# Turning and squaring the last four token tiles by channel chunk in a two-layer WKV/MoE kernel

## The chip, the cores and the metric

The kernel runs on one core of a Trainium2 chip. The core has a matrix engine (PE, with its weight loads shown apart as PEld), a vector engine (DVE), an activation engine (ACT), a general engine (POOL), and SP, which here only issues transfers. Each engine works through a queue of its own in order, and waits on semaphores that the others raise. The metric is the time of one execution on the device in microseconds (us); lower is better.

## What is computed

Input `x` is 4 x 512 x 512 (2048 tokens of 512 channels). Two layers follow one another, each a bidirectional WKV mixing and then a mixture of experts with a shared expert, each added to `x`. Cut to what matters here, the first layer is:

```python
# WKV: two decaying scans over time of exp(k) and exp(k)*v, then
num = nf + nb - ekv + euk * vf
den = df + db - ek + euk
z   = sigmoid(r) * (num / max(den, 1e-8)) * (0.8 + 0.2 * tf)
# experts
h      = z * rsqrt(mean(z * z, axis=-1) + 1e-6) * rms_weight
probs  = softmax(h @ router_w)                       # 8 experts
topv, topi = top_k(probs, 2)
moe    = sum of the two chosen experts, weighted by topv / sum(topv)
shared = silu(h @ sw_gate) * (h @ sw_up) @ sw_down
x      = x + moe + shared
```

The second layer has the same WKV and 32 experts, 6 chosen per token. The change lies in the passage of layer 0 from WKV to experts: it concerns `mean(z * z)` and `h @ router_w` of the last 512 tokens.

## The kernel before

The tokens are cut into four blocks of 512 (`b`), each into four tiles of 128 (16 tiles in all, `NT`), and the channels into four chunks of 128 (`c`). A *unit* `n` is one chunk of one block, 16 in all, worked on in the transposed layout (channels on partitions, tokens along the row). All queues have an order written out by hand: within an engine, instructions run in the order of the program text.

The main loop (line 697) has one pass per unit. For unit 15, the last, it issues the following.

- `mid(15)` (463): multiplications and four scans on DVE.
- `sums(14)` and, behind the loop, `sums(15)` (473): eight matmuls on PE, for `den` and `num`, and three activations on ACT that form `r`, the reciprocal of `den`.
- `back(14)` and, behind the loop, `back(15)` (486): four DVE operations that finish a unit's `z` in `zT`.
- `route_pos(2)` (578): two small matmuls of block 2 into the bank `pos2`. `route_slots(2)` (604), at the end of the pass on DVE, computes slot numbers from it (`slot_numbers`; lines 368 and 377 read the bank), and `write_slots(2, 8)` sends eight indirect writes on POOL.
- The shared expert of tiles 6, 7 and 8: `share_up` (PE), `share_silu` (ACT), `share_hid` (DVE).

Behind the loop come the router's steps for block 3 (lines 781 to 855). `last_channels` (787) adds one chunk to the logits `lgb` (line 789) and transposes that chunk of each tile in `pz` (line 791). `squares` (795) squares a range of columns of a tile on ACT and sums each token's squares into a column of `parts`. `share_turn(6)`, `share_down(6)` and `share_put(6)` turn the hidden rows of tile 6, multiply them by the down weights, and write the rows out. `lgT` is the logits' copy in SBUF, which PE turns back into token rows (line 821). Then `route_v`, `route_max`, `route_top`, `route_pos`, `route_pay` and `route_slots` compute the routing of block 3 on DVE with short steps on ACT and PE. `row_out` (515) copies a tile's rows and writes them to `z0d`. `write_slots` sends the last eight writes, `read_table` reads the finished table, and the experts' loop (`routed`, 872) gathers its rows by that table. Pieces of the shared expert for tiles 7 to 12 are laid between these steps.

Matmul results lie in eight PSUM banks handed out under tags:

```python
    banks.update(pool=ps, tr=2, den=2, num=1, g=2, pl=1)
```

A bank asked for under a tag is given once a bank of that tag has been read for the last time; the instruction that first writes it waits for this. In the kernel before, `pz` of tiles 12 and 13 take both `tr` banks and are turned and squared chunk by chunk (chunks 0 to 2 together, chunk 3 after `back(15)`); tiles 14 and 15 take the `num` bank and a `g` bank, and are turned whole (line 814) and squared whole after chunk 3. The single `pl` bank was last used by `pos2`; the two `g` banks by the shared expert's tiles 7 and 8.

Of the kernel before, what the change touches and what calls it, by code (L numbers as in the profile page):

```python
# [19 lines left out]
P = 128  # L20
# [13 lines left out]
def adaln_ffn_kernel(  # L34
# [26 lines left out]
    nc = tc.nc  # L61
    B, S, D = x.shape
# [4 lines left out]
    NC = D // P  # L67
    TB = S // P
    NT = T // P
# [17 lines left out]
    zT = big.tile([P, NC, T], F32, name="zT")  # L87
# [9 lines left out]
    def bank(tag, name):  # L97
        return banks["pool"].tile([P, 512], F32, tag=tag, name=name, bufs=banks[tag])


    ident = const.tile([P, P], F32, name="ident")
# [325 lines left out]
    def zcols(n):  # L427
        b, c = units[n]
        return zT[:, c, b * S : (b + 1) * S]
# [43 lines left out]
    def sums(n):  # L473

        b, c = units[n]
        den, num = bank("den", f"den{n}"), bank("num", f"num{n}")
        for p, m, (d, o) in zip((den, num), (ident, nfac[:, b, :]), mids.pop(n)):
            nc.tensor.matmul(p, m, d, start=True, stop=False)
            nc.tensor.matmul(p, m, o, start=False, stop=True)
        r = wk.tile([P, S], F32, tag="r", name=f"r{n}")  # L480
        nc.scalar.activation(r, den, AF.Relu, bias=neg_min)
        nc.scalar.activation(r, r, AF.Ln, bias=pos_min)
        nc.scalar.activation(r, r, AF.Exp, scale=-1.0)
        mids[n] = den, num, r

    def back(n):

        den, num, r = mids.pop(n)
        t = wk.tile([P, S], F32, tag="t", name=f"t{n}", bufs=1)
        nc.vector.scalar_tensor_tensor(t, den, DEN_MIN, r, ALU.max, ALU.mult)  # L490
        nc.vector.scalar_tensor_tensor(t, t, 2.0, r, ALU.subtract, ALU.mult)
        nc.vector.tensor_tensor(t, num, t, ALU.mult)
        nc.vector.tensor_tensor(zcols(n), zcols(n), t, ALU.mult)
# [147 lines left out]
    def share_turn(t, ph=None):  # L641
        if ph is None:
            ph = bank("tr", f"sph{t}")
        for f, _ in CH0:
            nc.tensor.transpose(ph[:, f : f + P], shared_hid[t][:, f : f + P], ident)
        hT = spool.tile([P, F0], F32, tag="hT", name=f"shT{t}")
        nc.scalar.copy(hT, ph[:, :F0])
        shared_hid[t] = hT

    def share_down(t, tag=None, po=None):  # L650
        dv, hT = shared0[2], shared_hid.pop(t)
        if po is None:
            po = bank(tag, f"so{t}")
        for j, (f, _) in enumerate(CH0):
            nc.tensor.matmul(po, hT[:, f : f + P], dv[:, j, :], start=(j == 0), stop=(j == len(CH0) - 1))
        shared_up[t] = po
# [40 lines left out]
    for n in range(NU):  # L697
        b, c = divmod(n, NC)
# [81 lines left out]

    bl = NB - 1
    lgb = bank("den", "lgb")
    pz = {t: bank("tr", f"pz{t}") for t in (NT - 4, NT - 3)}
    parts = wk.tile([P, 2, TB], F32, name="ssq_parts", bufs=1)
    nc.vector.memset(parts, 0.0)

    def last_channels(cs):
        for c in cs:
            nc.tensor.matmul(lgb[:E0], rout[:, c, :], zcols(bl * NC + c), start=(c == 0), stop=(c == NC - 1))
            for t, p in pz.items():  # L790
                nc.tensor.transpose(p[:, c * P : (c + 1) * P], zT[:, c, t * P : (t + 1) * P], ident)
# [3 lines left out]
    def squares(t, lo, hi, part):  # L795
        nc.scalar.activation(
            sq[:, lo:hi], pz[t][:, lo:hi], AF.Square, accum_out=parts[:, part, t - bl * TB : t - bl * TB + 1]
        )

    last_channels((0, 1))  # L800
    sums(NU - 1)
    last_channels((2,))
    for t in pz:
        squares(t, 0, D - P, 0)
    po = bank("g", "so_6")
    share_turn(6, po)
    back(NU - 1)
    share_down(6, po=po)
    last_channels((NC - 1,))
    lgT = wk.tile([E0, S], F32, tag="lgT", name="lgT_last", bufs=1)  # L810
    for t, tag in ((NT - 2, "num"), (NT - 1, "g")):
        pz[t] = bank(tag, f"pz{t}")
        for c in range(NC):
            nc.tensor.transpose(pz[t][:, c * P : (c + 1) * P], zT[:, c, t * P : (t + 1) * P], ident)
    squares(NT - 4, D - P, D, 1)
    squares(NT - 3, D - P, D, 1)
    nc.scalar.copy(lgT, lgb[:E0])
    squares(NT - 2, 0, D, 0)
    squares(NT - 1, 0, D, 0)
    for i in range(TB):  # L820
        nc.tensor.transpose(lgb[:, i * E0 : (i + 1) * E0], lgT[:, i * P : (i + 1) * P], ident[:E0, :E0])
    routes[bl] = lgb
# [425 lines left out]
    with tc.manual_schedule(  # L1248
# [6 lines left out]
        f, m = FCH[LAST]  # L1255
# [13 lines left out]
        for n in range(2 * NB):  # L1269
            b, t = n // 2, 2 * n + TB  # L1270
# [26 lines left out]
    for h in range(NHALF):  # L1297
# [3 lines left out]
        for b in range(NB):  # L1301
# [12 lines left out]
            for i in range(TB):  # L1314
                t = b * TB + i
                po = bank("tr", f"o{n}_{i}")
# [50 lines left out]
```

## Time and profile before

| what | value |
|---|---|
| median of 3 runs | 1504.74 us (1502.43 to 1507.55) |
| the profiled execution | 1499.05 us |
| its span in the trace | 1497.3 us |
| PE busy over the span | 93% |
| mean granted PE clock | 0.981 of full |
| DVE busy | 46% |
| ACT busy | 27% |
| POOL busy | 38% |
| start of the first logits matmul of block 3 (line 789) | 186.90 us |
| start of the first expert matmul (line 971) | 237.20 us |

The times are of the device. The table's last two rows bracket the stretch that the change touches: some 50 us out of 1497. Before it lies the WKV of layer 0, after it the experts of layer 0, then layer 1. Positions in the trace are counted from the start of the span. In the timelines of the profile, a row gives start, duration, engine, line, operation, output and inputs, count, and in brackets how long the engine was idle before it and who released it; matmuls overlap, so a row's duration is a little longer than its distance to the next.

### The profile page before, as it was taken

The page shows a single profiled execution, that of the slowest core. Times are in us where ns is not written, and L with a number is a line of the kernel's source. Part 1 is how long each engine was busy: PE and PEld are TensorE (multiplying, and loading weights), DVE is VectorE, ACT ScalarE, POOL GpSimd, SP SyncE. Part 2 cuts the span into 40 slices and gives each one's busy share as a digit, 9 for nine tenths or more (in the row PEclk, how much of TensorE's full clock was granted, in tenths as well). Part 3 has the DMA queues.
Part 4 walks back from the last instruction along what each step waited for, and adds up shares of the span by engine and source line. Part 5 has one row for each costly group of instructions (what it writes and reads, how often), then busy time and mean ns, then how long its engine had stood idle before and what let it go on. Part 6 is the DMA issues. An engine that isn't in the chain of part 4 may idle for free. (4 is left out here: it accounts for less than half of the span.)

```text
span 1497.3 us, 16067 instructions
## 1 busy us (share of the span) xinstructions
PE 1388.2 (93%) x4927; PEld 820.1 (55%) x4927; DVE 692.6 (46%) x1260; ACT 398.3 (27%) x962; POOL 573.6 (38%) x564
## 2 busy tenths in 40 slices
PE   5788888988788799999999999999999999999997
PEld 3455456766556454444445555555555555555554
DVE  7999949999980358511112222222222222222221
ACT  5666544444344251000001111111111111111110
POOL 1010245666564001555543343434343344343322
PEclk8999999999999999999999999999999999999999
DMA  8311216464545731010136654666456575546442
GB/s 301 99 54 51 78 58 188 77 132 99 131 104 124 244 132 52 1 58 29 56 110 187 153 142 115 169 170 194 103 131 182 142 231 155 142 129 165 111 96 40
DMA packets 118188, 184.71 MB, mean 123 GB/s; under 512 B 19864, under 2 KB 64940, under 8 KB 118040
## 3 DMA queue, kind: packets, MB, share of 16 engines
q1 hardware_dynamic: 82216, 125.28, 24.7%
q0 software_dynamic: 35296, 56.63, 20.2%
q8 instruction: 66, 1.08, 0.3%
q10 hardware_dynamic: 528, 1.05, 0.2%
q14 instruction: 82, 0.67, 0.1%
HBM read 151.02 MB, written 52.64 MB: 136 GB/s over the span
## 5 line engine op out<-in xcount | busy, mean ns | idle before, releaser
L946 PE MATMUL pout<-w,hT 128*128 128x512 f32 (+1 forms) x432 | 200.4, 596 | 1.3 <-DVE hT L939 0.8
L951 POOL DMA_INDIRECT out_dram<-kA,put x52 | 83.1, 1597 | 279.2 <-DVE kA L950 147.9
L905 POOL DMA_INDIRECT acc<-z1d,put x119 | 123.7, 1039 | 123.1 <-PE pza L918 63.2
L987 DVE SCALAR_TENSOR_TENSOR hrow<-pup,tab,sgt 128x352 f32<-128x352 f32 x84 | 49.1, 584 | 249.7 <-issue 127.4
L398 POOL DMA_INDIRECT table<-pay,r1sloti x96 | 95.1, 991 | 172.3 <-ACT sg L1309 111.7
L950 DVE COPY kA<-pout 128x512 f32<-128x512 f32 x84 | 58.1, 692 | 176.0 <-PE pout L946 164.1
L971 PE MATMUL pgate<-w,kA 128*128 128x352 f32 x416 | 132.8, 462 | 6.0 <-PEq L1032 5.9
L975 PE MATMUL pup<-w,kA 128*128 128x352 f32 x416 | 131.6, 459 | 0.0
L946 PEld LDWEIGHTS pout<-w,hT 128*128 128x128 f32 (+1 forms) x432 | 76.6, 191 | 67.6 <-issue 53.8
L986 ACT ACTIVATE sgt<-pgate 128x352 f32<-128x352 f32 x84 | 39.0, 464 | 250.5 <-PE pgate L971 245.4
L971 PEld LDWEIGHTS pgate<-w,kA 128*128 128x128 f32 x416 | 75.3, 190 | 49.8 <-issue 16.4
L918 PEld LDWEIGHTS pza<-ident,acc 128*128 128x128 f32 x584 | 72.3, 142 | 51.3 <-issue 33.5
L975 PEld LDWEIGHTS pup<-w,kA 128*128 128x128 f32 x416 | 77.4, 190 | 39.7 <-issue 0.2
L918 PE MATMUL pza<-ident,acc 128*128 128x128 f32 x584 | 87.4, 275 | 10.6 <-DMA acc<-z0d,put 8.5
L398 POOL DMA_INDIRECT table<-r0pay,r0sloti x32 | 34.7, 1085 | 158.8 <-DVE r0sloti L389 110.5
L928 ACT COPY kA<-pza 128x256 f32<-128x256 f32 x103 | 38.3, 372 | 205.8 <-DVE kA L927 156.7
L905 POOL DMA_INDIRECT acc<-z0d,put x51 | 68.1, 1335 | 58.4 <-PE pgate L971 18.6
L946 PE MATMUL pout<-zT,hT 128*128 128x512 f32 (+1 forms) x192 | 87.8, 592 | 0.0
L1153 PE MATMUL g<-zT,w 128*128 128x512 f32 (+1 forms) x192 | 86.5, 593 | 0.0
L1153 PE MATMUL u<-zT,w 128*128 128x512 f32 (+1 forms) x192 | 86.3, 592 | 0.0
L1318 PE MATMUL o<-w,kA 128*128 128x512 f32 (+1 forms) x192 | 84.5, 593 | 0.0
L971 PE MATMUL pgate<-zT,kA 128*128 128x352 f32 x256 | 81.3, 460 | 2.0 <-PEq L1032 2.0
(301 smaller groups left out, 2205.3 us busy)
## 6 DMA issues: line engine op xcount, KB each, us to landing
w<-in_L_ffn_w_dram SPq DMA_DIRECT2D x44, 704.0 KB, 5.8
zT<-in_L_ffn_w_dram SPq DMA_DIRECT2D x20, 704.0 KB, 5.8
w<-in_L_ffn_w_dram SPq DMA_DIRECT2D x22, 512.0 KB
zT<-in_L_ffn_w_dram SPq DMA_DIRECT2D x10, 512.0 KB
w<-in_L_ffn_w_dram SPq DMA_DIRECT2D x22, 192.0 KB, 8.6
acc<-in_x_dram SPq DMA_DIRECT2D x4, 1024.0 KB, 9.1
xa<-acc SPq DMA_DIRECT2D x4, 1024.0 KB
z0d<-zr SPq DMA_DIRECT2D x16, 256.0 KB, 2.0
```

Of the source, the lines that this page charges most:

```text
L398: ins = nc.gpsimd.indirect_dma_start(out=table, out_offset=bass.IndirectOffsetOnAxis(ap=sloti[:, t, j : j + 1], axis=0), in_=pay[:, t, j, ...
L905: nc.gpsimd.indirect_dma_start(out=rows(e, s), out_offset=None, in_=zd, in_offset=bass.IndirectOffsetOnAxis(ap=put_at[:, e * NS + s : e * ...
L918: nc.tensor.transpose(pza[which][:, c * P : (c + 1) * P], rows(e, s)[:, c * P : (c + 1) * P], ident)
L946: nc.tensor.matmul(po, hT[:m, j, :], dv[:m, j, :], start=(j == 0), stop=(j == nf - 1))
L950: nc.vector.tensor_copy(row, po)
L951: nc.gpsimd.indirect_dma_start(out=outs(n), out_offset=bass.IndirectOffsetOnAxis(ap=at, axis=0), in_=row, in_offset=None, bounds_check=T - ...
L971: nc.tensor.matmul(pg, zt[:, c, :], gv[:, c, :], start=(c == 0), stop=(c == NC - 1))
L975: nc.tensor.matmul(pu, zt[:, c, :], uv[:, c, :], start=(c == 0), stop=(c == NC - 1))
L986: nc.scalar.activation(sgt, pg, AF.Silu)
L987: nc.vector.scalar_tensor_tensor(hrow, pu, tab[:, col, 1:2], sgt, ALU.mult, ALU.mult)
L1153: nc.tensor.matmul(p[: m + more], wv[:, c, f : f + m + more], zT[:, c, b * S : (b + 1) * S], start=(c == 0), stop=(c == NC - 1),)
L1318: nc.tensor.matmul(po, hid[:m, j, i * P : (i + 1) * P], dv[:m, j, :], start=(j == 0), stop=(j == len(FCH) - 1))
```

## The change

```diff
     lgb = bank("den", "lgb")
-    pz = {t: bank("tr", f"pz{t}") for t in (NT - 4, NT - 3)}
+    pz = {bl * TB + i: bank(g, f"pz{bl * TB + i}") for i, g in enumerate(("tr", "tr", "pl", "g"))}
...
     last_channels((0, 1))
     sums(NU - 1)
     last_channels((2,))
+    po = bank("g", "so_6")
+    share_turn(6, po)
     for t in pz:
         squares(t, 0, D - P, 0)
-    po = bank("g", "so_6")
-    share_turn(6, po)
     back(NU - 1)
+    last_channels((NC - 1,))
     share_down(6, po=po)
-    last_channels((NC - 1,))
     lgT = wk.tile([E0, S], F32, tag="lgT", name="lgT_last", bufs=1)
-    for t, tag in ((NT - 2, "num"), (NT - 1, "g")):
-        pz[t] = bank(tag, f"pz{t}")
-        for c in range(NC):
-            nc.tensor.transpose(pz[t][:, c * P : (c + 1) * P], zT[:, c, t * P : (t + 1) * P], ident)
-    squares(NT - 4, D - P, D, 1)
-    squares(NT - 3, D - P, D, 1)
     nc.scalar.copy(lgT, lgb[:E0])
-    squares(NT - 2, 0, D, 0)
-    squares(NT - 1, 0, D, 0)
+    for t in pz:
+        squares(t, D - P, D, 1)
```

All four tiles of the last block are now in `pz` from the start, in banks `tr`, `tr`, `pl` and `g`, and each call of `last_channels` transposes its chunk of all four. Each tile is squared in two pieces: chunks 0 to 2 (384 columns), then chunk 3 (128 columns). The turning of tile 6's hidden rows, with its copy on ACT, stands ahead of the first squares; chunk 3 of the logits and transposes stands ahead of tile 6's down product; the copy `lgT` stands ahead of all four last squares. The number of transposes is the same (16); the squares are eight activations in place of six. No transfer is added, removed or moved past another.

## The prediction

> **What bounds the kernel now.** I read the page first: PE is busy 93% of the span, and the chain that ended last runs, from the end back, through the experts of layer 1.
>
> ```profile
> PE 1388.2 (93%) x4927; PEld 820.1 (55%) x4927; DVE 692.6 (46%) x1260; ACT 398.3 (27%) x962; POOL 573.6 (38%) x564
> ```
>
> That is an average. The change touches 50 us around the hand-over from WKV to experts in layer 0, so I took the timeline of each engine there (PE first, then POOL), asking which wait ends last.
>
> ```profile
> 230.46 1.98 POOL L905 DMA_INDIRECT acc<-z0d,put  x1 [0.28 <-PE so L655]
> ...
> 235.61 1.08 PE L918 MATMUL pza<-ident,acc 128*128 128x128 f32 x4 [5.16 <-DMA acc<-z0d,put]
> ```
>
> PE has done all its shared-expert work and stands idle 5.16 us for the first gather. Backwards: gather, table read (226.08), eight slot writes one after another (214.16 to 224.14), slot numbers on DVE (to 213.88), their start behind `share_hid(9)` at 210.08, and before that the routing of block 3, which starts when the last square is summed (DVE line 824 at 201.61). Behind the gather PE runs almost without gaps to the end. **So the hand-over is on the path**: what delays the slot writes delays the end one for one, and PE work that fits into the 5.16 us is free.
>
> Now the stretch itself, in the timelines of PE, ACT and DVE:
>
> ```profile
> 186.90 1.03 PE L789 MATMUL lgb<-zT,rout 128*8 128x512 f32 x2
> 187.86 0.44 PE L791 MATMUL pz<-ident,zT 128*128 128x128 f32 x2
> 188.22 1.02 PE L789 MATMUL lgb<-zT,rout 128*8 128x512 f32 x2
> 189.18 0.44 PE L791 MATMUL pz<-ident,zT 128*128 128x128 f32 x2
> 189.46 1.02 PE L478 MATMUL den<-v,ident 128*128 128x512 f32 x2
> ...
> 195.82 1.98 PE L655 MATMUL so<-w,shT 128*128 128x512 f32 x4 [1.22 <-ACT shT L647]
> 197.73 1.02 PE L789 MATMUL lgb<-zT,rout 128*8 128x512 f32 x2
> ```
> ```profile
> 191.93 0.18 DVE L377 TENSOR_SCALAR r0addr<-pos 128x32 f32<-128x32 f32 x1
> ...
> 195.76 0.69 DVE L493 TENSOR_TENSOR zT<-zT,t 128x512 f32<-128x512 f32 x1
> 201.61 0.16 DVE L824 TENSOR_TENSOR ssq_parts<-ssq_parts 128x4 f32<-128x4 f32 x1 [5.16 <-ACT sq L796]
> ```
>
> Two things are to be seen. `zT` is complete at 196.45 but the last logits start at 197.73, behind tile 6's down product: 1.28 us that the change wants. And block 2's positions, in the only `pl` bank, are read last by DVE line 377, until 192.11. That is four microseconds after PE is through with the first transposes.
>
> **The change, part by part.**
>
> *The bank `pl` (adds a wait).* Tile 14's first transpose comes right behind those of tiles 12 and 13, at 188.3, and must wait for `pos2` to be read: 192.11, plus 0.06 as line 581 follows its mask on DVE (207.55 to 207.61), so **192.17**. Everything behind it on PE waits: tile 15, chunk 1, and `sums(15)`, which ACT's `r`, DVE's `back(15)` and thus all the routing wait for. DVE itself isn't held up: by 192.11 it needs nothing from behind the stall. The `tr` banks and tile 15's `g` bank (hidden rows of tile 7 read by 182.2) are free in time; the other `g` bank, for `so_6`, is free at 191.5.
>
> *PE before `sums(15)`.* After the wait: two transposes (0.28, 189.18 to 189.46), logits (0.96, 188.22 to 189.18), four transposes (0.50; the row gives 0.28 for two, and eight of line 814 follow each other at 0.11). Sum 1.74: `sums(15)` at 193.91 instead of 189.46, **+4.45**, at full clock.
>
> *The clock.* Here the trace has a rule of its own. The windows view, cut at the edges at which the granted clock changes (PE busy first, granted clock third from last), says:
>
> ```profile
> 177.91:181.32 3.41, 0.79 (x4) 0.59 (x4) 2.79 (x20) 1.66 (x3) 0.00 (x0) 1.00 0.00 0
> 181.32:184.73 3.41, 2.89 (x7) 2.35 (x8) 3.41 (x8) 0.00 (x0) 0.00 (x0) 0.50 0.00 0
> ...
> 229.11:232.52 3.41, 1.35 (x4) 0.28 (x2) 3.34 (x4) 0.89 (x2) 3.05 (x2) 1.00 0.37 143
> 232.52:235.93 3.41, 0.32 (x2) 0.35 (x3) 3.31 (x6) 0.00 (x0) 2.58 (x3) 0.50 0.74 234
> ...
> 474.86:478.28 3.42, 1.46 (x7) 1.34 (x8) 0.00 (x0) 0.13 (x2) 1.61 (x1) 1.00 0.36 32
> 478.28:481.69 3.41, 3.41 (x19) 2.75 (x18) 0.00 (x0) 1.60 (x5) 0.00 (x0) 1.00 0.32 59
> ```
>
> With 0.79 or 1.35 us of work in a window the next ran at half clock; with 1.46 it did not. The Trainium skill ("TensorE: Matmul & The Clock Gate", Part 1, What's actually happening) says that the clock halves after at least one *idle* window of about 3.4 us. In the changed kernel the window 188.15 to 191.56 keeps some 0.15 us of transposes, then nothing: by the page's words it isn't idle, the clock stays, and `sums(15)` is +4.45; by the rows it is far under 1.35, and 191.56 to 194.97 runs at half. I take the rows. From 192.17 the 2.80 us of half clock do 1.40 of the 1.74, the rest takes 0.34: `sums(15)` at 195.31, **+5.85**. The page calls the window free-running; then its edges fall elsewhere in other executions, but a gap of 3.87 us leaves less than 1.4 us of work in some window for about nine positions in ten. Ends: no loss, or one full window (1.71).
>
> I carry both clocks on (full / half).
>
> *Down to the last square.* From the start of `sums(15)` to the end of `back(15)` it is 6.99 (189.46 to 196.45): 200.90 / 202.30. Chunk 3 no longer stands behind the down product: 200.96 / 202.36, which recovers 1.22 of the 1.28. Its logits are done 1.06 later: 202.02 / 203.42. Is ACT free then? It does the copy of hidden rows 5.41 after `sums(15)` starts (0.30), then four squares of 384 columns at 0.545 (two from 194.31 to 195.40): free at 201.80 / 203.20. Yes, with 0.2 us to spare. Then `lgT` (0.47, 199.72 to 200.19) and four squares of 128 (0.335 each, two from 199.05 to 199.72, and 0.10 for the last read-out): line 824 at 203.99 / 205.39, **+2.38 / +3.78**. The removed whole squares (1.39 for two) are in this difference.
>
> *The down product, now behind chunk 3.* It costs PE 1.72 there (four at 0.43) before the logits are turned (0.34): `share_up(9)` at 204.48 / 205.88 in place of 200.67, +3.81 / +5.21. The routing is not held up by the turned logits, but by what comes later: `share_down(7)` ends at 210.86 / 212.26 in place of 207.05, and tile 7's output copy on ACT then starts at 210.92 / 212.32; before it started at 207.67, behind a row copy that waited 1.19 us for a transfer. Behind this copy stand the table load, `share_silu(9)`, and on DVE `share_hid(9)`, ahead of the slot numbers. This lane is later than the routing itself, so the slot writes move by **+3.2 / +4.6**.
>
> *Costed at nothing:* `pl` in `route_pos(3)` must wait for tile 14's row copy on ACT, about 211.4, and PE gets there after 212; the `g` banks of `so7` and `so8` come free by copies on ACT 3 us and 1 us ahead. PE's shared work ends near 235.5 instead of 230.35, before the first gather at 240. SP and POOL queues keep their order.
>
> Sum at half clock: +4.6 on 1499.05 gives 1503.7 for the profiled execution (1497.3 of span and 1.75 around it). That execution was faster than all three timed runs, so I set the difference on their median: **1504.74 + 4.6 = 1509.3**.
>
> **Rivals.**
> 1. *The wait without the half clock* (+3.2, 1507.9): as above by the page's wording, or in executions whose windows fall so. Against it: the two rows with 0.79 and 1.35.
> 2. *No wait, and the change gains* (ends not slower). If `pos2` were read before PE comes to tile 14, only four more transposes precede `sums(15)` (0.50): `zT` is complete at 196.95, chunk 3's logits at 198.07, line 824 at 200.0 (-1.6), but `share_down(7)` ends only at 206.9, so the tile 7 copy moves by -0.7: 1504.0. Each microsecond of wait costs one, so this side decides below 0.7 us of wait; the rows have 3.87. For it: only that another bank might be at hand; the tag has one.
> 3. *Further windows fall.* The experts of layer 0 have five half-clock windows between 382 and 495 us at their gaps; shifting everything moves these gaps against the windows. Two more cost 3.4: +8.0, 1512.7. Against it: it may as well save two.
>
> **Chances.** Forecast 0.58, rival 1 0.18, rival 2 0.10, rival 3 0.14. A measurement of this kernel tells a change from none at about 0.3%, 4.5 us, right at my forecast. Slower: a little over half of the forecast, all of rival 3, little of rival 1: 0.51. Faster: a third of rival 2, and noise: 0.05. Same: 0.44. The range, 1503 to 1515, spans rival 2's edge to rival 3 with the scatter of the runs (2.5 us either way); the forecast's own is 1506 to 1513.
>
> **What would show it.** In the profile after: PE idle 3.5 to 4 us ahead of tile 14's first transpose, released by DVE near 192.1; half clock in the window after; `sums(15)` at 194 to 195.5; chunk 3 directly behind `back(15)`; line 824 at 204 to 205.5; the first slot write of block 3 at 217.4 to 218.8. No idle time there would make me wrong outright; a first write within 1 us of 214.16 would break the later lane.

## The result, and the profile after

| | before | after |
|---|---|---|
| median of 22 runs each | 1503.48 us (1499.06 to 1507.55) | 1507.37 us (1505.01 to 1513.96) |
| profiled execution, its span | 1499.05, 1497.3 us | 1507.03, 1505.2 us |
| ratio of the runs | | 1.0027, 95% interval 1.0018 to 1.0036 |

The changed kernel is slower by 0.27%, 3.9 us between the medians (2.7 to 5.4 us by the interval). By the bound that the forecast set itself, 0.3%, that is no change; by the interval it is a small loss. The forecast, 1509.3 us, lies 1.9 us above: some 1.3 us of that is its starting point (1504.74, the median of three executions, where 22 give 1503.48), the rest is the change (4.6 us forecast, 3.9 measured).

These are rows of the timeline of PE after, and three windows of the same profile (PE busy stands first, the granted clock third from last):

```profile
188.12 1.02 PE L789 MATMUL lgb<-zT,rout 128*8 128x512 f32 x2
189.07 0.44 PE L791 MATMUL pz<-ident,zT 128*128 128x128 f32 x2
192.76 0.41 PE L791 MATMUL pz<-ident,zT 128*128 128x128 f32 x2 [3.25 <-DVE r0addr L377]
193.10 1.52 PE L789 MATMUL lgb<-zT,rout 128*8 128x512 f32 x2
194.55 1.12 PE L791 MATMUL pz<-ident,zT 128*128 128x128 f32 x4
195.46 1.75 PE L478 MATMUL den<-v,ident 128*128 128x512 f32 x2
...
203.23 1.02 PE L789 MATMUL lgb<-zT,rout 128*8 128x512 f32 x2 [1.69 <-DVE zT L493]
...
240.81 0.65 PE L912 MATMUL pza<-ident,acc 128*128 128x128 f32 x4 [4.63 <-DMA acc<-z0d,put]
```
```profile
190.07:193.48 3.41, 0.72 (x3) 0.30 (x4) 3.06 (x12) 1.27 (x2) 0.00 (x0) 1.00 0.00 0
193.48:196.90 3.42, 3.42 (x8) 1.59 (x7) 0.27 (x3) 0.00 (x0) 2.23 (x3) 0.50 0.01 0
196.90:200.31 3.41, 3.41 (x9) 1.05 (x7) 0.07 (x1) 2.04 (x3) 2.67 (x3) 1.00 0.03 1
```

The wait stands where it was forecast, with its releaser by name: line 377 on DVE, the last read of `pos2`. In the two rows behind it the logits take 1.52 us in place of 1.02, and four transposes 1.12 in place of 0.66 (e1, below): the granted clock is 0.50 from 193.5 to 196.9. `sums(15)` starts at 195.46 and not at 189.46. Chunk 3 starts 0.06 us after `zT` is whole (202.48 + 0.69), as the change intends; but `zT` itself is whole 6.7 us later than before.

From the timeline of DVE after, then of POOL before and of POOL after:

```profile
202.48 0.69 DVE L493 TENSOR_TENSOR zT<-zT,t 128x512 f32<-128x512 f32 x1
206.36 0.16 DVE L818 TENSOR_TENSOR ssq_parts<-ssq_parts 128x4 f32<-128x4 f32 x1 [3.18 <-ACT sq L796]
...
215.66 0.48 DVE L638 SCALAR_TENSOR_TENSOR shr<-sg,rs,ssg 128x256 f32<-128x256 f32 x1 [2.56 <-ACT ssg L632]
```
```profile
193.57 0.98 POOL L398 DMA_INDIRECT table<-r0pay,r0sloti  x1 [29.33 <-DVE ssq_parts L785]
...
214.16 0.98 POOL L398 DMA_INDIRECT table<-r0pay,r0sloti  x1 [10.44 <-DVE counts L851]
```
```profile
194.06 0.98 POOL L398 DMA_INDIRECT table<-r0pay,r0sloti  x1 [29.31 <-DVE ssq_parts L785]
...
219.72 0.98 POOL L398 DMA_INDIRECT table<-r0pay,r0sloti  x1 [15.69 <-DVE counts L845]
```

The last sum of squares is 4.75 us later than before, and the first slot write of block 3 5.56 us later. Half a microsecond of that was there before the change comes in (block 2's first slot write at 194.06 in place of 193.57). I therefore use as the measure of the stretch **the time from block 2's first slot write to block 3's**: 20.59 us before (193.57 to 214.16), 25.66 after. PE still waits for the first gather, 4.63 us where it waited 5.16, so nearly all of the delay is passed on: PE goes on at 240.81 in place of 235.61, 5.20 us later. What is behind it varies more than the change is worth: from the gather to the shared expert's tail (PE line 627 at 483.70 before and 491.88 after) it is 248.1 us before and 251.1 after, and between 248 and 258 in all the profiles below. A single profile can therefore show the stretch, but not the loss in total time; for that the timed runs count.

### The profile page after: what moved, and what is told of

Read it like the earlier page. It is cut to its first block, busy times and chain, and to the rows that moved or that the text cites. A ratio compares the mean times of both kernels' runs of the same rounds, so it can differ in the third digit from the quotient of the medians.

```text
span 1505.2 us, 16071 instructions
## 1 busy us (share of the span) xinstructions
PE 1393.0 (93%) x4927; PEld 823.6 (55%) x4927; DVE 694.1 (46%) x1260; ACT 398.1 (26%) x966; POOL 572.6 (38%) x564
## 6 DMA issues: line engine op xcount, KB each, us to landing
w<-in_L_ffn_w_dram SPq DMA_DIRECT2D x22, 192.0 KB
```

## The experiments

Ratios are to the kernel before, with 95% intervals; "stretch" is the measure above, from one profile each.

| run | ratio | stretch, us |
|---|---|---|
| before, after | 1, 1.0027 (1.0018 to 1.0036) | 20.59, 25.66 |
| e1: positions copied out of `pl` | 0.9994 (0.9986 to 1.0003) | 21.52 |
| e2: `pl` alone, in the kernel before | 1.0024 (1.0016 to 1.0032) | 25.92 |
| e3: no tile in `pl` | 0.9995 (0.9985 to 1.0006) | 21.56 |
| e4: 28 transposes in the wait | 1.0045 (1.0028 to 1.0062) | 24.43 |
| e8: the same 28 elsewhere | 1.0047 (1.0031 to 1.0063) | 26.99 |
| e9: 3 products in the wait | 1.0023 (1.0015 to 1.0032) | 24.03 |
| e10: the same 3 elsewhere | 1.0022 (1.0010 to 1.0033) | 24.03 |
| e5: after, `share_hid(9)` late | 0.9999 (0.9987 to 1.0010) | 22.62 |
| e7: before, `share_hid(9)` late | 0.9989 (0.9980 to 0.9998) | 18.36 |
| e6: e1 and e5 together | 0.9981 (0.9971 to 0.9991) | 16.92 |

### Is it the wait for the bank?

**e1** lets ACT, idle at that time, copy block 2's positions to SBUF, so that `pl` is free early; `route_slots(2)` then reads the copy.

```diff
             share_silu(two)
             if n + 1 == NU:
+                pr, oh, pos = routes[b - 1]
+                posk = wk.tile([P, TB * E0], F32, tag="posk", name="posk", bufs=1)
+                nc.scalar.copy(posk, pos)
+                routes[b - 1] = pr, oh, posk
                 share_hid(one)
```

> The changed kernel, with block 2's positions copied from the pl bank to SBUF by ACT (128x32) between share_silu(7) and share_silu(8), so that the bank is free some ten microseconds before tile 14 needs it. Measure: the time from block 2's first slot write to block 3's first slot write, 20.59 us in the profile of before (193.57 to 214.16) and 25.66 in that of after (194.06 to 219.72). Theory A (the wait for the pl bank is the cost): no wait over 0.3 us ahead of tile 14's first transpose, no half clock behind it, 19.9 us (0.7 under before), ratio to before about 0.9995. Rival B (the new order and the eight squares cost: the down product behind chunk 3, the hidden rows' copy ahead of the squares): 23 us or more, ratio 1.0015 or more.

**e2** puts the wait, and nothing else of the change, into the kernel before.

```diff
-    pz = {t: bank("tr", f"pz{t}") for t in (NT - 4, NT - 3)}
+    pz = {t: bank(g, f"pz{t}") for t, g in ((NT - 4, "tr"), (NT - 3, "pl"))}
```

> The kernel before with one edit: tile 13 takes the pl bank in place of the second tr bank. Order, number of squares and everything else stay. Theory A: tile 13's first transpose waits for line 377 (3 to 4 us), sums(15) starts 4.1 us later at full clock or 5.5 at half, and here all that follows moves with it: 24.7 to 26.1 us from block 2's first slot write to block 3's (before 20.59), ratio 1.0027 to 1.0037. Rival B (order and squares cost): under 22 us, ratio under 1.001.

**e3** leaves tile 14 out of the chunk-wise work, and with it the bank.

```diff
-    pz = {bl * TB + i: bank(g, f"pz{bl * TB + i}") for i, g in enumerate(("tr", "tr", "pl", "g"))}
+    pz = {bl * TB + i: bank(g, f"pz{bl * TB + i}") for i, g in ((0, "tr"), (1, "tr"), (3, "g"))}
...
     share_down(6, po=po)
+    whole = NT - 2
+    pz[whole] = bank("num", f"pz{whole}")
+    for c in range(NC):
+        nc.tensor.transpose(pz[whole][:, c * P : (c + 1) * P], zT[:, c, whole * P : (whole + 1) * P], ident)
...
     for t in pz:
-        squares(t, D - P, D, 1)
+        squares(t, 0 if t == whole else D - P, D, 1)
```

> The changed kernel, but tile 14 is turned and squared whole behind tile 6's down product, in the num bank as before; tiles 12, 13 and 15 by chunk. No tile in pl. Theory A: no wait; chunk 3 directly behind back(15), 1.2 us earlier than before, given back by tile 14's transposes behind the down product and its whole square: 20.2 to 20.8 us between the two first slot writes, ratio 0.9995 to 1.0005. Rival B: the down product's place costs by itself: 22 us or more, ratio over 1.001.

The ratios settle it. With the wait taken away and all the reordering kept (e1), the loss is gone: 0.9994, interval clear of after's. With the wait alone (e2) it is all there: 1.0024. The order and the eight squares (rival B) cost nothing that shows. Rows of PE in e2:

```profile
188.93 1.02 PE L789 MATMUL lgb<-zT,rout 128*8 128x512 f32 x2
189.88 0.33 PE L791 MATMUL pz<-ident,zT 128*128 128x128 f32 x1
193.57 0.30 PE L791 MATMUL pz<-ident,zT 128*128 128x128 f32 x1 [3.35 <-DVE r0addr L377]
...
195.61 1.92 PE L478 MATMUL den<-v,ident 128*128 128x512 f32 x2
```

One of the two transposes goes at 189.88, the other, into `pl`, 3.35 us of idle PE later. The same in e1, where no row behind `share_up(8)` (the first) waits:

```profile
181.79 6.75 PE L627 MATMUL sg<-w,zT 128*128 128x256 f32 x16 [1.71 <-DVE shr L638]
188.48 1.03 PE L793 MATMUL lgb<-zT,rout 128*8 128x512 f32 x2
189.44 0.66 PE L795 MATMUL pz<-ident,zT 128*128 128x128 f32 x4
190.02 1.02 PE L793 MATMUL lgb<-zT,rout 128*8 128x512 f32 x2
190.98 0.66 PE L795 MATMUL pz<-ident,zT 128*128 128x128 f32 x4
191.47 1.02 PE L478 MATMUL den<-v,ident 128*128 128x512 f32 x2
```

But both e1 and e3 missed my figure for the stretch: 21.52 and 21.56 us where 19.9 and 20.2 to 20.8 were expected. The first row shows why: `share_up(8)`, ahead of everything, took 6.75 us here and 5.13 in the profile of before, 1.62 us more. That led to the next question.

### How long is the wait, and where is the clock?

All kernels run the same PE instructions up to block 3's first logits. Still `share_up(8)` takes 5.1 to 5.3 us, 5.8 to 6.0 or 6.6 to 6.8 in their profiles. Here are its rows in before, after and e10:

```profile
181.84 5.13 PE L627 MATMUL sg<-w,zT 128*128 128x256 f32 x16 [1.71 <-DVE shr L638]
```
```profile
182.34 5.84 PE L627 MATMUL sg<-w,zT 128*128 128x256 f32 x16 [1.48 <-DVE shr L638]
```
```profile
182.09 6.67 PE L627 MATMUL sg<-w,zT 128*128 128x256 f32 x16 [1.70 <-DVE shr L638]
```

The granted clock is 0.50 from 181.3 to 184.7 in the first, from 179.8 to 186.7 in the second and from 181.3 to 188.1 in the third. So PE comes to the wait between 188.2 and 190.2, while the wait's end is set by DVE. Two repeats looked at this.

> The kernel before once more, for a second profile. Nine profiles of kernels with the same code up to the first logits of block 3 show share_up(8) taking 5.1, 5.8 or 6.7 us, as the half-clock window falls. Theory A: the first logits start between 186.8 and 188.9 us, and if share_up(8) takes 5.8 or more, the two first slot writes stand 21.2 to 22.3 us apart in place of 20.59: the profile on which the forecast was built had the early arrival, and so the longer wait. Otherwise: 20.6 us whatever share_up(8) takes.

> The changed kernel once more, for a second profile. Theory A: the wait ahead of tile 14's first transpose ends with line 377 on DVE whatever share_up(8) takes, so 3.0 to 4.0 us of idle PE, half clock in the window after it, and 25.2 to 27 us between the two first slot writes.

The repeat of the kernel before took 5.96 us for `share_up(8)` and 21.11 for the stretch, 0.1 short of what was expected but on its side. The repeat of after took 5.22, waited longer (3.88 us), and gave 27.04, 0.04 above what was expected. Its PE rows and windows:

```profile
188.18 0.44 PE L791 MATMUL pz<-ident,zT 128*128 128x128 f32 x2
192.50 0.66 PE L791 MATMUL pz<-ident,zT 128*128 128x128 f32 x2 [3.88 <-DVE r0addr L377]
193.09 1.88 PE L789 MATMUL lgb<-zT,rout 128*8 128x512 f32 x2
194.90 1.12 PE L791 MATMUL pz<-ident,zT 128*128 128x128 f32 x4
195.80 1.92 PE L478 MATMUL den<-v,ident 128*128 128x512 f32 x2
197.51 1.67 PE L479 MATMUL den<-euk,ident 128*128 128x512 f32 x2
```
```profile
188.56:191.98 3.42, 0.06 (x1) 0.00 (x0) 3.21 (x7) 1.88 (x3) 0.00 (x0) 1.00 0.00 0
191.98:195.39 3.41, 2.89 (x7) 0.89 (x8) 1.34 (x9) 0.00 (x0) 1.29 (x2) 0.50 0.00 0
195.39:198.80 3.41, 3.41 (x7) 1.76 (x7) 0.00 (x0) 0.00 (x0) 2.63 (x3) 0.50 0.02 1
```

Half clock from 192.0 to 198.8: two windows and not one, and it reaches into `sums(15)`. To take the clock out, I filled the wait with PE work whose result is not used, first as 28 transposes (**e4**), with a control that has them elsewhere (**e8**):

```diff
             for t, p in pz.items():
+                if c == 0 and t == NT - 2:
+                    for _ in range(28):
+                        nc.tensor.transpose(pz[NT - 1][:, :P], zT[:, c, (NT - 1) * P : NT * P], ident)
                 nc.tensor.transpose(p[:, c * P : (c + 1) * P], zT[:, c, t * P : (t + 1) * P], ident)
```

> The changed kernel, with 28 idle transposes of tile 15's chunk 0 (into its own bank, overwritten by the real one) ahead of tile 14's first transpose: 3.1 us of PE work inside the wait, which should end before the bank is free. The wait stays, the idle window goes. Theory A with the half clock as part of the cost: no half clock behind the wait, sums(15) starts 1.8 us after tile 14's first transpose in place of 2.70 in the profile of after, 24.0 to 24.5 us between the two first slot writes (after 25.66), ratio 1.0017 to 1.0020. Rival C (the clock plays no part in the cost): 25.4 us or more, ratio 1.0027 as after.

> The changed kernel with the same 28 idle transposes as in the run that kept PE busy, but behind the pc matmul, where PE waits for an ACT copy, so that all later code is displaced by as many instructions while the wait for the pl bank stays idle. Question: why that run lost time though its first slot write came earlier. Theory L (the displaced code costs: the loop's branches into unread code fall elsewhere): 25.2 to 26.2 us between the first slot writes as in after, half clock behind the wait, and yet 1.0048 to 1.0054, slower than the run that kept PE busy by about 0.0008, what the clock is worth. Rival M (keeping PE busy itself costs later): 1.0027 to 1.003, as after.

Then as three products of 128x512 (**e9**), again with a control (**e10**):

```diff
+                    for _ in range(3):
+                        nc.tensor.matmul(pz[NT - 1], ident, zcols(bl * NC), start=True, stop=True)
...
     nc.tensor.matmul(pc[:, :E0], ones, past[:, NT, :], start=True, stop=True)
+    for _ in range(3):
+        nc.tensor.matmul(lgb, ident, zcols(bl * NC), start=True, stop=True)
```

> The clock again, with less displaced code: in the changed kernel three idle 128x512 products (some 2.6 us, twelve PE instructions in place of 56) into tile 15's bank ahead of tile 14's first transpose. Theory A (half clock part of the cost): no half clock behind the wait, 24.0 to 24.8 us between the two first slot writes, ratio 1.0015 to 1.002 if twelve instructions leave the loop's gaps where they are. Rival C (the clock plays no part in the time): as its control below, within 0.0005.

> Control for the run with three idle products: the same three behind the pc matmul, the wait left idle. Theory A: half clock behind the wait, 25.5 to 27 us between the two first slot writes, ratio 1.0027 (no displaced gap), 0.0008 or more above the other. Rival C: no difference between the two.

In the profiles of e4 and e9 the clock stays whole behind the wait and the stretch is 24.43 and 24.03, as theory A had it. (In e4 PE came late, and the 28 transposes kept it until 192.76, half a microsecond longer than line 377, which ended at 192.18.) The surprise is the control e10: its wait was left idle, and yet

```profile
189.64 0.44 PE L791 MATMUL pz<-ident,zT 128*128 128x128 f32 x2
192.51 0.41 PE L791 MATMUL pz<-ident,zT 128*128 128x128 f32 x2 [2.43 <-DVE r0addr L377]
...
194.30 1.02 PE L478 MATMUL den<-v,ident 128*128 128x512 f32 x2
```
```profile
188.09:191.50 3.41, 1.99 (x7) 0.53 (x6) 3.24 (x6) 2.67 (x4) 0.00 (x0) 1.00 0.00 0
191.50:194.92 3.42, 2.41 (x10) 1.18 (x11) 1.80 (x11) 0.42 (x1) 0.98 (x1) 1.00 0.00 0
```

full clock, and 24.03 us, where I expected half clock and 25.5 to 27. Here `share_up(8)` had taken 6.67 us, PE came late, and the 2.43 us of idle time fell across an edge between two windows, which kept 1.99 and 2.41 us of work. So the half clock lengthens the stretch in some executions and not in others. Its share of the *timed* loss was not shown: e9 and e10 stand at 1.0023 and 1.0022, my expectation of 0.0008 between them did not come out, and the intervals could hide it. Rival C is not refuted for the time.

Nor is e4's total what I expected. Its stretch was shorter than after's, its time longer by 0.18%, and e8, with the same number of instructions put elsewhere, is as slow, so it does not look like the filled wait. But these are six and five runs; their intervals begin at 1.0028 and 1.0031, and after's ends at 1.0036, so that even the extra loss is not beyond doubt. Theory L, displaced code, gave e8's ratio a hair too high (1.0048 to 1.0054 against 1.0047), its distance to e4 too large (0.0008 against 0.0002) and its stretch too short (25.2 to 26.2 against 26.99, since PE arrived early). In the timelines of PE in before and in e4, these are the rows that waited longest for "issue", that is for nothing that the profile shows:

```profile
382.58 3.65 PE L971 MATMUL pgate<-w,zgT 128*128 128x256 f32 x8 [4.24 <-issue]
```
```profile
484.98 3.56 PE L968 MATMUL pgate<-w,zgT 128*128 128x256 f32 x8 [6.24 <-issue]
```

A gap at an expert's boundary near 383 in before is gone in e4, and one of 6.24 us stands at another boundary near 485 (in e8 5.34 us at 488.01). All ten profiles of kernels without added PE instructions have such a gap between 380 and 393 us, of 3.62 to 7.95 us; with twelve more (e9 and e10) the longest is 1.59 us, near 435. So the place of the gap goes with the number of PE instructions ahead of it. The time does not go with its length: the longest is that of e6, the fastest kernel, and e9 and e10, nearly without it, stand at 1.0023 and 1.0022. What fills these gaps was not tried, and why e4 and e8 are slow stays open.

### Which lane sets the slot writes?

**e5**, **e6** and **e7** move one DVE instruction, `share_hid(9)`, behind the slot numbers; e5 in the changed kernel, e7 in the one before, e6 together with e1.

```diff
     route_top(bl)
-    share_hid(early)
     route_pos(bl)
...
     write_slots(bl, TB * 2)
+    share_hid(early)
```

> The changed kernel, with share_hid(9) on DVE moved behind the slot numbers and slot writes of block 3. Theory A says that in the changed kernel the first slot write of block 3 hangs on the lane share_down(6), share_up(9), share_down(7), tile 7's copy, table load, share_silu(9), share_hid(9), and not on the routing: DVE stands idle 2.56 us (213.10 to 215.66 in the profile of after) ahead of share_hid(9) itself (0.40). So 22.7 us between the two first slot writes in place of 25.66, ratio to before 1.0007 to 1.0009. Rival D (the routing sets the slot writes, the lane is only beside it): over 25 us, ratio 1.0027.

> Both edits together in the changed kernel: positions copied out of the pl bank early, share_hid(9) behind the slot writes. Theory A: from 21.52 us (the run with the copied positions) the 2.18 us of idle DVE and 0.4 of share_hid go: 18.9 us, ratio 0.9977. Rival D: 21 us or more, ratio 0.9994.

> The kernel before with share_hid(9) behind the slot writes, nothing else. Theory A: DVE stood idle 1.72 us ahead of it, plus 0.4: 18.5 us in place of 20.59 if the clock falls as in the profile of before, up to 19.8 if it falls as in the other profiles; ratio 0.9986. Rival D: no less than 20.5, ratio 1.0000.

The stretches are 22.62, 16.92 and 18.36 us; rival D, which had over 25, 21 or more and 20.5 or more, falls. (e5's ratio, 0.9999, came out below the expected 1.0007 to 1.0009, which its interval still holds.) In e6, the timeline of DVE has no wait for another engine from the end of `route_top` (line 575) to the slot numbers, and that of PE has the next bound:

```profile
206.50 0.77 DVE L575 TENSOR_TENSOR past<-past,r0mask 128x8 f32<-128x8 f32 x4
207.19 0.22 DVE L592 TENSOR_TENSOR r0prod_w<-r0oh,r0pr 128x64 f32<-128x64 f32 x1
...
210.41 0.17 DVE L389 CAST r0sloti<-r0slotf 128x8 int32<-128x8 f32 x1
210.49 0.48 DVE L638 SCALAR_TENSOR_TENSOR shr<-sg,rs,ssg 128x256 f32<-128x256 f32 x1
```
```profile
226.52 3.60 PE L655 MATMUL so<-w,shT 128*128 128x512 f32 x8
230.61 0.63 PE L916 MATMUL pza<-ident,acc 128*128 128x128 f32 x4 [0.49 <-DMA acc<-z0d,put]
```

PE waits 0.49 us for the first gather: from here on, less routing time can buy no more than that without less PE work. **e6 beats both kernels**: 1501.67 us, 0.9981 of before (0.9971 to 0.9991). Its stretch beat the expected 18.9 because its `share_up(8)` took 5.11 us; the 18.9 was reckoned from e1, which had 6.75. In total time e6 is not clear of e7 (0.9989, 0.9980 to 0.9998), which keeps the old order. But their profiles have the same early arrival of PE (`share_up(8)` 5.11 and 5.14), and there e6's stretch is 1.44 us the shorter: with the wait and the later lane out of the way, the reordering does gain about the 1.28 us that it was made for.

## Why the prediction was right, point by point

The mechanism was right; that the sum came so close owes something to luck, as the second point shows.

- **The wait for `pl`** (192.17 as its end, 3.87 us, all behind it held up): right in place, releaser and effect, shown by e1 and e2. Its end was 192.12 to 193.15 in the profiles of kernels with after's order and an idle wait. Its length was taken from one execution in which PE arrived early; the profiles have 3.94, 3.88, 3.26, 3.25 and 2.43.
- **The half clock** (2.80 us of it, "about nine positions in ten"): right in kind in both profiles of after, wrong in its size. I varied the window's edges and kept PE's arrival fixed, but the clock that is granted earlier decides how long `share_up(8)` takes and so when PE comes to the wait. Sorted by this, the profiles say:

| `share_up(8)`, us | stretch before | stretch after's order | half clock behind the wait |
|---|---|---|---|
| 5.1 to 5.2 | 20.59 (before) | 27.04 (a2), 26.99 (e8) | two windows |
| 5.8 to 6.0 | 21.11 (b2) | 25.66 (after) | one window |
| 6.7 | none taken | 24.03 (e10) | none |

  The two differences are +6.45 and +4.55 us; for the third, e3, which has no wait and is as fast as before, gives 21.56, and so about +2.5. My +4.6 was worked out for the first row, the early arrival, where the profiles have +6.45: half clock for 6.8 us, and not for 2.80. What the clock alone is worth there shows in e9, which has the same early arrival (`share_up(8)` 5.26) and the clock whole: 24.03, or +3.44, where I had +3.2 at full clock. So the half clock made 3.0 us of the +6.45, and I had put it at 1.4. That my sum agrees with the second row, a later arrival that I had not reckoned with, is luck. The runs' 3.9 us would fit a mixture of the three rows, but how often each occurs was not measured. The mis-sized term is the half clock, with the arrival that goes with it; the mechanism is not.

  Nor is the edge that I read off three rows (half clock after 1.35 us of work, not after 1.46) a sharp one. The same profile of before has 1.64 us followed by half clock:

```profile
24.30:27.72 3.42, 1.64 (x12) 1.33 (x13) 3.25 (x5) 3.13 (x6) 0.00 (x0) 1.00 1.05 413
27.72:31.13 3.41, 3.41 (x6) 1.35 (x5) 3.34 (x6) 2.12 (x3) 1.38 (x3) 0.50 1.04 394
```

  The forecast did not hang on it: the windows of the wait held 0.72 us of work (after) and 0.06 (a2).
- **From `sums(15)` to the end of `back(15)`, 6.99 us:** exact in e1 (191.47 to 197.77 + 0.69). In after it was 7.71, since the half clock reached into the first products.
- **Chunk 3 behind `back(15)`, ACT free 0.2 us before its logits:** right, with nothing to spare. The four squares took 2.44 us (201.85 to 204.29) and not 2.18. In after the last 384-column square ends at 204.28, and the logits' copy starts at 204.29, where 203.23 + 1.06 puts the end of the logits too.
- **The later lane through tile 7's copy and `share_hid(9)`:** right. DVE idled 2.56 us for it, and e5 took it out: 25.66 to 22.62 where 22.7 was expected.
- **The signs given:** the wait of 3.25 us lay below the 3.5 to 4 forecast, `sums(15)` (195.46) inside its range; the last sum of squares, at 206.36, came after 204 to 205.5, and the first slot write, at 219.72, after 217.4 to 218.8. Both are late for the clock's reason above and the 0.49 us by which block 2's writes were later.
- **Costed at nothing:** the slack ahead of the first gather held (4.63 us of PE idle time left).
- **The rivals:** rival 1 (no half clock) is what e10's profile shows, the only one of five profiles with after's order and an idle wait (after, a2, e5, e8, e10); that is no argument against the 0.18 given to it. Rival 2 (no wait) needed another kernel: e1 is it, 0.9994 where 1504.0 on 1504.74 had been reckoned. Rival 3 did not show: between 382 and 495 us there are four half-clock windows in after and three in a2, where before and b2 have five and seven.

## What to carry to other kernels

Before a tile is moved into a bank, look up in the trace who reads that bank last and when: a queue that works in order turns one early request into a wait for all behind it, and a 0.2 us copy by an idle engine can release the bank. A gain of a microsecond on one engine counts only if the lane that ends last is the one shortened; here a single instruction moved off it took 2.2 us off the stretch in the old order (e7), while the reordering freed of its wait showed no gain clear of noise (e1). And when a forecast rests on when an engine arrives, take the arrival from several profiles: one execution can be the early one.

## What the runs showed of the hardware

- The half clock fell differently from profile to profile of the same code, and that shows twice: sixteen matmuls ahead of the wait took 5.1 to 6.8 us in different profiles of the same code, and the less time they took, the longer the idle time behind them (3.9 us against 2.4) and the half clock after it (6.8 us against none). In after, a window of 3.41 us with 0.72 us of PE work, and so not an idle one, was followed by half clock.
- Fifty-six PE instructions more, in either of two places of the stretch, stood at 1.0045 (1.0028 to 1.0062) and 1.0047 (1.0031 to 1.0063) where after stands at 1.0027 (1.0018 to 1.0036); in e4 they ran inside a wait. With twelve more it was 1.0023 and 1.0022. The cause is not known.
